# Hybrid attention and MLP on one core: double places for dequantized pieces, layer norm by turns with them, and zero products beside the first block's last maxima

## The chip, the cores and the metric

The kernel runs on one core of one Trainium2 chip. The metric is the device time of one execution in microseconds (us), the median of several. Before the change it is 1871.18 us (three runs, 1871.15 to 1873.65).

A core has five engines that run side by side, each with its own queue of instructions in a fixed order: PE (matrix products, with its weight loads PEld beside them), DVE (vectors), ACT (activations), POOL (vectors, and the issue of some DMAs) and SP (issue of DMAs). They wait for each other by semaphores. Products land in PSUM, from which DVE and ACT read.

## The reference

A layer stack on x of 2048 rows and 256 columns, in float32. The same packed MLP weights are used twice:

```python
x = x + attn_a(layernorm(x), Wq, bq, Wk, bk, Wv, bv, Wo, bo)   # rotary, 16 heads, 4 key heads, causal
x = x + ffn(layernorm(x), gate, up, down)
x = x + attn_b(layernorm(x), Wq, Wk, Wv, Wo)                   # 16 heads, causal
x = x + ffn(layernorm(x), gate, up, down)

def ffn(x, ...):                 # weights: 4-bit codes, two in an int32, times a scale per 32
    Wg, Wu, Wd = dequant_nvfp4(...)               # value = LUT[code] * scale
    gate, up = x @ Wg.T, x @ Wu.T                 # 2048 features
    gelu = tanh(0.79788 * (gate + 0.044715 * gate**3)) * gate * 0.5 + gate * 0.5
    return (gelu * up) @ Wd.T
```

Softmax is computed with the maximum of each row subtracted, so a row's maxima over all its keys must be known before its exponentials.

## The kernel before, in words

**Stages.** First attention, MLP, second attention, MLP. The 2048 rows are four blocks b of 512 rows. An attention goes through 16 units (b, g): block b of queries, group g of four heads, in the order (0,0), (0,1) ... (3,3). Unit n computes the values (exponentials and products with v) of its own queries, and beside them the row maxima of unit n+1.

**A unit's main steps** come from value_steps (L819): for each of 4(b+1) tiles of keys kt two pairs p. pair (L845) puts the scores of two heads into a ps_s buffer: two matmuls L853 that add the negative maxima mT, two matmuls L858 with the keys; on the diagonal a mask (L733), held back until the next step that settles it (settle, L738); then ACT's exp (L870). values (L824) multiplies the exponentials of the tile before with v (L838) into ps_av. There are three ps_s buffers, one ps_av and one ps_m.

**Its side steps** are woven between the main steps (weave, L43; blend, L61, merges two lists by their relative places). They are:
- the maxima of the next unit (max_steps, L747): for each step a pair of matmuls L758 into a ps_s buffer, and DVE's reduction L770; on the diagonal a mask held back in the same way. Then gather (L782 to L793, DVE) and at the unit's end turn: four matmuls L806 into ps_m, which ACT copies to mT (L812). For units up to (1,0) turn begins with four matmuls of zeros into ps_m that nobody reads (L802).
- the out projection of the block before (out_steps, L912) and the preparation of the block after (prep_steps, L438: layer norm, projections, rotary sums on POOL at L519, key loads issued by POOL at L705, query loads issued by SP at L719).
- in the first attention, `extra`: dequantizing, 72 steps, shared out over units 4 to 15 (none to those with g = 3 but the last). Units 4, 5 and 6 get 6, 5 and 5 steps, units 8 to 10 get 6, 5 and 5, units 12 to 14 get 6, 5 and 5, and the last unit, which has no maxima, gets 24.
- in the last unit, `beside`: 13 steps of layer norm for the first block of the MLP (Mlp.prep_steps, L1003): four of statistics (L295, L296 on DVE), one root (L300 on DVE, L302 on POOL), four norms (L310, DVE), four turns (two PE transposes L1016 into ps_m, an ACT copy L1017). They stand behind all of `extra`. The second attention has no `extra`, so there they stand alone.

**Dequantizing** is in 12 pieces (dequant_steps, L319): eight for gate and up, which go straight to wg and wu in SBUF, and four for down, which go to DRAM (wd_kept). A piece is six steps of unpack (L323):
1. load: SP loads the codes dq_q (L330), POOL issues eight loads of the scales dq_s (L339).
2. lowest: POOL copies the low bytes of dq_q to dq_b (L344).
3. and 4. move 0 and move 1: DVE takes dq_b apart (L355, L357 or L359, L361).
5. and 6. scaled 0 and scaled 1: DVE multiplies with dq_s (L370); for a down piece the last one also issues a store on SP (L399).

Every tile of the pool has one buffer. So the load of piece i waits on SP until lowest of piece i-1 has read dq_q, and on POOL until scaled 1 of piece i-1 has read dq_s.

**The MLP** begins with the matmuls L1040 on the turned layer norm xnT and the weights wg and wu. Its down weights wd are loaded from wd_kept (L1032) and used after the 16 feature steps of a block.

Of the kernel before, what the change touches and what calls it, by code (L numbers as in the profile page):

```python
# [9 lines left out]
F32 = mybir.dt.float32  # L10
# [4 lines left out]
I32 = mybir.dt.int32  # L15
# [6 lines left out]
P = 128  # L22
# [8 lines left out]
TB = 512  # L31
# [29 lines left out]
def blend(a, b):  # L61

    keyed = [((n + 0.5) / len(a), 0, n, f) for n, f in enumerate(a)]
    keyed += [((n + 0.5) / len(b), 1, n, f) for n, f in enumerate(b)]
    return [f for *_, f in sorted(keyed, key=lambda k: k[:3])]


def cut(steps, n):

    while 0 < n < len(steps) and getattr(steps[n - 1], "open", False):  # L70
        n += 1
    return steps[:n], steps[n:]
# [8 lines left out]
def tile_hybrid_layers(  # L81
# [25 lines left out]
    nc = tc.nc  # L107
# [20 lines left out]
    def ps_m():  # L128
        return psum.tile([P, 512], F32, tag="m", name="ps_m")
# [59 lines left out]
    nothing = const.tile([P, TB], BF16, tag="nothing", name="nothing")  # L189
    nc.vector.memset(nothing, 0.0)  # L190
    sel = const.tile([P, 2, P], BF16, tag="sel", name="sel")
# [127 lines left out]
    def dequant_steps(pool):  # L319

        def unpack(src, scale, results, done):  # L323
            held = {}
            n = TB // 4
            mag, sgn = 0x1C1C1C1C, 0x80808080

            def load():
                q = pool.tile([P, TB], I32, tag="dq_q", name="dq_q")
                nc.sync.dma_start(out=q, in_=src) if len(src.shape) == 2 else nc.sync.dma_start(  # L330
                    out=q.rearrange("p (c h) -> p c h", h=D), in_=src
                )
                s = pool.tile([P, TB], F32, tag="dq_s", name="dq_s")
                for r in range(8):
                    rows = s[16 * r : 16 * (r + 1), :]
                    row = scale(r)
                    if len(row.shape) == 3:
                        rows = rows.rearrange("p (c h) -> p c h", h=D)
                    nc.gpsimd.dma_start(out=rows, in_=row.broadcast_to(list(rows.shape)))  # L339
                held["q"], held["s"] = q, s  # L340

            def lowest():
                b8 = pool.tile([P, TB], U8, tag="dq_b", name="dq_b")
                nc.gpsimd.tensor_copy(  # L344
                    b8, held["q"].bitcast(U8).rearrange("p (n k) -> p n k", k=4)[:, :, 0]
                )
                held["w"] = b8.bitcast(U32)

            def move(k):

                w = held["w"]
                t = pool.tile([P, n], U32, tag=f"dq_t{k}", name="dq_t")
                v = pool.tile([P, n], U32, tag=f"dq_v{k}", name="dq_v")
                shift = (ALU.logical_shift_left, ALU.logical_shift_right)[k]
                nc.vector.tensor_scalar(t, w, 2, mag, shift, ALU.bitwise_and)  # L355
                if k == 0:
                    nc.vector.tensor_scalar(v, w, 4, sgn, shift, ALU.bitwise_and)  # L357
                else:
                    nc.vector.tensor_scalar(v, w, sgn, None, ALU.bitwise_and)  # L359
                e = pool.tile([P, n], U32, tag=f"dq_e{k}", name="dq_e")  # L360
                nc.vector.tensor_tensor(e, t, v, ALU.bitwise_or)  # L361
                held[k] = e

            def scaled(k):
                to = results()[k]
                code, sc = held[k].bitcast(FP8), held["s"]
                if len(to.shape) == 3:
                    code = code.rearrange("p (c h) -> p c h", h=D)
                    sc = sc.rearrange("p (c h) -> p c h", h=D)
                nc.vector.scalar_tensor_tensor(to, code, 64.0, sc, ALU.mult, ALU.mult)  # L370
                if k == 1 and done:
                    done()

            return [
                load, lowest, lambda: move(0), lambda: move(1), lambda: scaled(0), lambda: scaled(1)
            ]

        steps = []
        for k in range(MLP // TB):
            cols = slice(k * TB, (k + 1) * TB)  # L380
            for src, sc, w in ((gate_p, gate_s, wg), (up_p, up_s, wu)):
                steps += unpack(
                    src[:, cols], lambda r, sc=sc, cols=cols: sc[r : r + 1, cols],
                    lambda w=w, cols=cols: (w[:, 0, cols], w[:, 1, cols]), None,
                )
        d_p = down_p.rearrange("(c p) h -> p c h", p=P)
        d_s = down_s.rearrange("(c r) h -> r c h", r=8)
        for k in range(4):
            cc = slice(2 * k, 2 * k + 2)
            held = {}  # L390

            def results(held=held):
                if not held:
                    held["t"] = pool.tile([P, 4, D], F32, tag="dq_d", name="dq_d")
                w = held["t"].rearrange("p (c b) h -> p b c h", b=2)
                return w[:, 0], w[:, 1]

            def done(held=held, k=k):
                nc.sync.dma_start(out=wd_kept[:, 4 * k : 4 * k + 4, :], in_=held["t"])  # L399

            steps += unpack(
                d_p[:, cc, :], lambda r, cc=cc: d_s[r : r + 1, cc, :], results, done
            )
        return steps


    class Attention:
# [535 lines left out]
        def run(self, extra, beside):  # L943


            units = [(b, g) for b in range(NB) for g in range(NG)]


            room = [0 if n < NG else 9 if n + 1 == len(units) else 2 * (g < 3 or b + 1 == NB)
                    for n, (b, g) in enumerate(units)]  # L950
            shares = [-(-len(extra) * sum(room[: n + 1]) // sum(room)) for n in range(len(units))]
            given, ending, ahead = 0, [], []
            for n, (b, g) in enumerate(units):
                lead, more = [], []
                if g == 0 and b > 0:
                    more += self.out_steps(b - 1)
                if g == 0 and b + 1 < NB:
                    ahead = self.prep_steps(b + 1)

                    third = len(ahead) / 3  # L960
                    few = [round(third) - (1 if b else 2), round(third) + 1, len(ahead)]
                if g < 3 and b + 1 < NB:
                    part, ahead = cut(ahead, few[g])
                    if g == 2:

                        part[6:6] = [lambda b=b: self.load_q(b + 1, 0)]
                    more += part
                if shares[n] > given:
                    more = blend(more, extra[given : shares[n]])
                    given = shares[n]  # L970
                if n == 0 and self.after:
                    lead, more = self.after[:2], self.after[2:] + more
                elif n + 2 < len(units) and g != 2:
                    self.load_q(*units[n + 2])
                maxima, turn = [], None
                if n + 1 < len(units):
                    maxima, turn = self.max_steps(*units[n + 1])
                else:
                    more += beside
                steps, end, divide = self.value_steps(b, g)  # L980

                for at, step in zip((0, 2), ending):
                    scored, *summed = steps[at] if isinstance(steps[at], tuple) else (steps[at],)
                    steps[at] = (scored, step, *summed)
                if turn:
                    scored, summed = steps[-1]
                    steps[-1] = (turn, scored, summed)
                first = len(maxima) * 3 // len(steps)
                weave(steps[:3], lead + maxima[:first])
                weave(steps[3:], blend(maxima[first:], more) if maxima else more, rest=3)  # L990
                ending = [end, divide]
            end()
            return [divide] + self.out_steps(NB - 1)
# [93 lines left out]
    with tc.tile_pool(name="wk1", bufs=2) as wk, tc.tile_pool(name="kv1", bufs=1) as kv:  # L1087
        at.wk = at.qpool = wk
        with tc.tile_pool(name="init", bufs=1) as pool:
            zeros = pool.tile([P, TB], BF16, tag="zeros", name="zeros")  # L1090
# [13 lines left out]
            steps, turn = at.max_steps(0, 0)  # L1104
# [12 lines left out]
        with tc.tile_pool(name="dq", bufs=1, reuse_waits="tile") as pool:  # L1117
            left = at.run(dequant_steps(pool), mlps[0].prep_steps(0))
    first_w.close()
    at = Attention(False, wqkv_second)  # L1120
    with tc.tile_pool(name="kv20", bufs=1, reuse_waits="tile") as kv0, tc.tile_pool(
        name="wk2", bufs=2, reuse_waits="tile"
# [7 lines left out]
        steps, turn = at.max_steps(0, 0)  # L1130
# [60 lines left out]
```

## Time and profile before

| what | us |
|---|---|
| median of three runs | 1871.18 |
| the profiled execution: its own time | 1874.91 |
| the profiled execution: span from first to last instruction | 1873.1 |
| busy: PE / DVE / ACT / POOL | 1779.5 / 1124.8 / 806.5 / 240.3 |
| mean granted PE clock (1 is full) | 0.983 |
| DVE's reductions for the maxima, L770, 640 of them | 659.0 |
| exponentials, L870, 640 of them | 571.5 |
| first attention: unit (0,3) / last unit, from the L806 matmuls before it | from 107.40 / from 572.67 |
| second attention: unit (0,3) / last unit, from the L806 matmuls before it | from 1039.76 / from 1490.07 |

How to read it: a timeline row gives start, length, engine, line, operation, output and inputs with sizes, and how often; brackets give the engine's idle time just before and what ended it. A row of a stretch gives its length, then the busy time of PE, PEld, DVE, ACT and POOL with the number of instructions, then the granted PE clock, the share of DMA and GB/s. PE's matmuls overlap, so its busy time is an upper estimate. All times are us from the start of the span.

### The profile page before, as it was taken

What the parts mean: (1) busy time and instruction counts of PE and PEld (TensorE: products, weight loads), DVE (VectorE), ACT (ScalarE), POOL (GpSimd) and SP (SyncE); (2) the same over time, 40 slices, a digit from 0 to 9 for tenths busy, and PEclk for the clock granted to TensorE, in tenths of its full rate; (3) what the DMA queues carried; (4) which work ended last, traced back from release to release, by engine and by line L of the source; (5) the groups of instructions that cost most, each with busy time, mean ns of one, the idle gap of its engine ahead of it and who ended that gap; (6) DMA issues with size and microseconds to landing.
All of it is one profiled execution on the core that took longest, in us unless ns stands there. A gap on an engine that the chain in (4) does not pass through costs nothing. (4 is left out here: it accounts for less than half of the span.)

```text
span 1873.1 us, 31992 instructions
## 1 busy us (share of the span) xinstructions
PE 1779.5 (95%) x13534; PEld 929.9 (50%) x13534; DVE 1124.8 (60%) x1679; ACT 806.5 (43%) x1071; POOL 240.3 (13%) x444
## 2 busy tenths in 40 slices
PE   8889999999999899999998899999999999999999
PEld 4444444444443465747464444444444444756656
DVE  4567787788884444363545667766877716353442
ACT  2334556556667322132314355565566663131221
POOL 4121201200003111012101010010000001011110
PEclk9879999999999899999999899999999999999999
DMA  5131300200002100003104122022000010000000
GB/s 136 52 80 24 86 24 24 63 24 24 19 12 75 57 6 1 1 0 77 47 0 91 46 57 69 13 63 63 13 13 2 1 46 1 12 3 9 6 6 12
DMA packets 41887, 63.45 MB, mean 34 GB/s; under 512 B 13712, under 2 KB 20752, under 8 KB 41488
## 3 DMA queue, kind: packets, MB, share of 16 engines
q1 hardware_dynamic: 33104, 45.41, 7.9%
q0 software_dynamic: 7680, 15.48, 4.9%
q8 instruction: 106, 1.74, 0.4%
q10 hardware_dynamic: 960, 0.52, 0.1%
q14 instruction: 37, 0.30, 0.1%
HBM read 43.45 MB, written 17.83 MB: 33 GB/s over the span
## 5 line engine op out<-in xcount | busy, mean ns | idle before, releaser
L770 DVE TENSOR_REDUCE mx<-ps_s 128x2 f32<-128x1024 f32 (+3 forms) x640 | 659.0, 1061 | 224.0 <-PE ps_s L733 116.5
L870 ACT ACTIVATE e<-ps_s 128x1024 f32<-128x1024 f32 (+3 forms) x640 | 571.5, 897 | 412.9 <-PE ps_s L858 234.0
L838 PE MATMUL ps_av<-e,v 128*32 128x256 f32 (+1 forms) x4608 | 366.8, 387 | 0.4 <-ACT e L870 0.4
L858 PE MATMUL ps_s<-qT,kT 64*128 64x512 f32 (+3 forms) x1280 | 339.4, 523 | 0.0
L758 PE MATMUL ps_s<-kT,qT 64*128 64x512 f32 (+3 forms) x1280 | 269.0, 425 | 32.2 <-ACT e L870 14.3
L853 PE MATMUL ps_s<-mT,sel 64*128 64x512 bf16 (+3 forms) x1280 | 231.2, 355 | 27.5 <-ACT mT L812 11.0
L1040 PE MATMUL ps_s<-xnT,wg 128*128 128x512 f32 x512 | 240.9, 593 | 0.0
L1040 PE MATMUL ps_s<-xnT,wu 128*128 128x512 f32 x512 | 240.6, 592 | 0.0
L853 PEld LDWEIGHTS <-sel 64*128 64x128 bf16 x1280 | 74.9, 93 | 253.7 <-issue 243.3
L758 PEld LDWEIGHTS ps_s<-kT,qT 64*128 64x128 f32 x1280 | 129.4, 189 | 137.7 <-ACT e L870 67.6
L1046 ACT ACTIVATE t<-ps_s 128x512 f32<-128x512 f32 x128 | 76.3, 596 | 244.2 <-PE ps_s L1040 243.7
L1048 DVE TENSOR_TENSOR t<-ps_s,t 128x512 f32<-128x512 f32 x128 | 88.1, 688 | 141.2 <-POOL t L1047 139.2
L1049 ACT ACTIVATE t<-t 128x512 f32<-128x512 f32 x128 | 80.6, 629 | 198.9 <-DVE t L1048 198.9
L1040 PEld LDWEIGHTS ps_s<-xnT,wu 128*128 128x128 f32 x512 | 97.3, 190 | 122.5 <-issue 122.5
L1047 POOL TENSOR_SCALAR t<-t 128x512 f32<-128x512 f32 x128 | 79.1, 618 | 548.0 <-ACT t L1046 544.4
L1040 PEld LDWEIGHTS ps_s<-xnT,wg 128*128 128x128 f32 x512 | 95.1, 190 | 104.2 <-issue 102.5
L838 PEld LDWEIGHTS ps_av<-e,v 128*32 128x32 f32 x4608 | 94.9, 109 | 104.2 <-issue 87.9
L1050 DVE SCALAR_TENSOR_TENSOR t<-t,ps_s 128x512 f32<-128x512 f32 x128 | 88.0, 687 | 89.0 <-ACT t L1049 89.0
L858 PEld LDWEIGHTS ps_s<-qT,kT 64*128 64x128 f32 x1280 | 129.8, 198 | 0.0
L1065 PE MATMUL ps_m<-wd,inter 128*128 128x256 f32 x512 | 114.5, 380 | 0.0
L1065 PE MATMUL ps_av<-wd,inter 128*128 128x256 f32 x512 | 114.5, 380 | 0.0
L1065 PEld LDWEIGHTS ps_av<-wd,inter 128*128 128x128 f32 x512 | 96.7, 190 | 17.1 <-issue 4.5
(145 smaller groups left out, 1206.6 us busy)
## 6 DMA issues: line engine op xcount, KB each, us to landing
qT<-h SPq DMA_DIRECT2D x248, 64.0 KB, 2.2
kT<-h POOLq DMA_DIRECT2D x88, 128.0 KB, 5.0
h<-high SPq DMA_DIRECT2D x24, 256.0 KB, 2.1
h<-low SPq DMA_DIRECT2D x24, 256.0 KB, 2.4
wd<-wd_kept SPq DMA_DIRECT2D x2, 2048.0 KB, 8.2
wd_kept<-dq_d SPq DMA_DIRECT2D x4, 512.0 KB, 2.7
out<-x SPq DMA_DIRECT2D x16, 128.0 KB, 1.7
x<-x SPq DMA_DIRECT2D x3, 512.0 KB, 7.8
```

The source lines that it names most:

```text
L758: nc.tensor.matmul(pt[:, r, :w], lhsT=self.qT[b, g][64 * r : 64 * r + 64, p, i * P : (i + 1) * P], rhs=self.key_rows(c, g, p, r, slice(0, w)),
L770: nc.vector.tensor_reduce(held["mx"][:, i, 2 * p : 2 * p + 2, c], pt[:, :, :w], AX.X, ALU.max)
L838: nc.tensor.matmul(held["av"][32 * j : 32 * j + 32, own], lhsT=self.vv[kt // NT][:, kt % NT, h * VW : h * VW + 32], rhs=es_[j // 2][:, j % ...
L853: nc.tensor.matmul(pt[:, r, q0:], lhsT=sel[64 * r : 64 * r + 64, p, :], rhs=self.mT[b, g][64 * r : 64 * r + 64, q0:], start=True, stop=False,)
L858: nc.tensor.matmul(pt[:, r, q0:], lhsT=self.key_rows(kt // NT, g, p, r, keys), rhs=self.qT[b, g][64 * r : 64 * r + 64, p, q0:], start=Fals ...
L870: nc.scalar.activation(e[:, :, q0:], pt[:, :, q0:], AF.Exp, scale=QK_SCALE)
L1040: nc.tensor.matmul(pt[:, k, :], lhsT=w[:, c, fc * P : (fc + 1) * P], rhs=self.xnT[b][:, c, :], start=(c == 0), stop=(c == 1),)
L1047: nc.gpsimd.tensor_scalar(t, t, GELU_A, 1.0, ALU.mult, ALU.add)
L1048: nc.vector.tensor_tensor(t, gate, t, ALU.mult)
L1049: nc.scalar.activation(t, t, AF.Tanh, scale=GELU_C)
L1050: nc.vector.scalar_tensor_tensor(t, t, 1.0, gate, ALU.add, ALU.mult)
L1065: nc.tensor.matmul(po[:, :D], lhsT=inter[:, fc, i * P : (i + 1) * P], rhs=wd[:, fc, :], start=(fc == 0), stop=(fc == NFC - 1),)
```

## The change

Three edits, all in how side steps are made and ordered.

1. dq_q and dq_s get two buffers each (4 KB more per partition), and dequant_steps no longer strings the pieces one after another: the load of piece i+1 is put ahead of lowest of piece i. There are still 72 steps, shared out as before, so every step but the loads moves back by one place. Load of piece i+1 now waits for piece i-1 to be done with its buffer.
2. In the last unit of an attention, layer norm (`beside`) is merged with the dequantizing steps by blend, not appended. In the second attention there is nothing to merge with.
3. In unit (0,3) of both attentions, eight steps `zeros` are merged among the 16 maxima of unit (1,0): each takes ps_m and does two matmuls of 128 by 512 zeros in bfloat16, which nobody reads. The four at L802 stay.

```diff
@@ unpack, load
-                q = pool.tile([P, TB], I32, tag="dq_q", name="dq_q")
+                q = pool.tile([P, TB], I32, tag="dq_q", name="dq_q", bufs=2)
...
-                s = pool.tile([P, TB], F32, tag="dq_s", name="dq_s")
+                s = pool.tile([P, TB], F32, tag="dq_s", name="dq_s", bufs=2)
@@ dequant_steps
-        steps = []
+        pieces = []
...
-                steps += unpack(
+                pieces.append(unpack(
...
+        steps = pieces[0][:1]
+        for piece, then in zip(pieces, pieces[1:] + [[]]):
+            steps += then[:1] + piece[1:]
         return steps
@@ Attention.run
+            def zeros():
+                pt = ps_m()
+                for _ in range(2):
+                    nc.tensor.matmul(
+                        pt, lhsT=sel[:, 0, :], rhs=nothing, start=True, stop=True
+                    )
...
                 else:
-                    more += beside
+                    more = blend(more, beside)
...
+                if (b, g) == (0, 3):
+
+                    maxima = blend(maxima[:-1], [zeros] * 8) + maxima[-1:]
                 first = len(maxima) * 3 // len(steps)
                 weave(steps[:3], lead + maxima[:first])
                 weave(steps[3:], blend(maxima[first:], more) if maxima else more, rest=3)
```

In the last unit of the first attention the order of the side steps was load 8, lowest 8, move, move, scaled, scaled, load 9 and so on to scaled 1 of piece 11, then layer norm. It is now scaled 1 of piece 7, statistics 0, load 9, lowest 8, statistics 1, move 0 of 8, move 1 of 8, statistics 2, scaled 0 of 8, statistics 3, scaled 1 of 8, load 10, root, lowest 9, move 0 of 9, norm 0, move 1 of 9, scaled 0 of 9, norm 1, scaled 1 of 9, load 11, norm 2, lowest 10, move 0 of 10, norm 3, move 1 of 10, scaled 0 of 10, turn 0, scaled 1 of 10, turn 1, lowest 11, move 0 of 11, turn 2, move 1 of 11, scaled 0 of 11, turn 3, scaled 1 of 11.

More of the change, by code (lines that the diff above doesn't have):

```diff
@@ L381, in dequant_steps @@
             for src, sc, w in ((gate_p, gate_s, wg), (up_p, up_s, wu)):
-                steps += unpack(
+                pieces.append(unpack(
                     src[:, cols], lambda r, sc=sc, cols=cols: sc[r : r + 1, cols],
                     lambda w=w, cols=cols: (w[:, 0, cols], w[:, 1, cols]), None,
-                )
+                ))
         d_p = down_p.rearrange("(c p) h -> p c h", p=P)
@@ L399, in done @@
                 nc.sync.dma_start(out=wd_kept[:, 4 * k : 4 * k + 4, :], in_=held["t"])
-            steps += unpack(
+            pieces.append(unpack(
                 d_p[:, cc, :], lambda r, cc=cc: d_s[r : r + 1, cc, :], results, done
-            )
+            ))
+        steps = pieces[0][:1]
+        for piece, then in zip(pieces, pieces[1:] + [[]]):
+            steps += then[:1] + piece[1:]
         return steps
```

## The prediction

> **What bounds the kernel now.** I read the page first, then where engines wait in the stretches that the change touches, then the timelines of PE and DVE there, then both last units side by side, and last the granted clock window by window.
>
> ```profile
> PE 1779.5 (95%) x13534; PEld 929.9 (50%) x13534; DVE 1124.8 (60%) x1679; ACT 806.5 (43%) x1071; POOL 240.3 (13%) x444
> ```
>
> PE sets the end nearly everywhere, so an edit pays only where PE idles or runs at a low clock. There are two such places in reach of the change. The first is the end of the first attention's last unit, block 3, group 3 (PE, timeline):
>
> ```profile
> 604.93 0.47 PE L858 MATMUL ps_s<-qT,kT 64*128 64x384 f32 x2
> 611.93 0.70 PE L1016 MATMUL ps_m<-ident,xn 128*128 128x128 f32 x2 [6.53 <-DVE xn L310]
> ...
> 623.66 1.98 PE L1040 MATMUL ps_s<-xnT,wg 128*128 128x512 f32 x4
> ```
>
> PE idles 6.53 us for a layer-norm result of DVE. DVE's timeline says why it is late:
>
> ```profile
> 587.33 0.23 DVE L355 TENSOR_SCALAR dq_t<-dq_b 128x128 uint32<-128x128 uint32 x1 [7.33 <-POOL dq_b L344]
> 596.10 0.23 DVE L355 TENSOR_SCALAR dq_t<-dq_b 128x128 uint32<-128x128 uint32 x1 [6.08 <-POOL dq_b L344]
> 605.28 0.23 DVE L355 TENSOR_SCALAR dq_t<-dq_b 128x128 uint32<-128x128 uint32 x1 [6.14 <-POOL dq_b L344]
> 607.89 0.42 DVE L295 BATCH_NORM_STATS2 stats<-x 128x6 f32<-128x256 f32 x1
> ...
> 611.47 1.38 DVE L310 TENSOR_SCALAR xn<-x,mv,rstd 128x256 f32<-128x256 f32 x4 [1.16 <-POOL rstd L302]
> ```
>
> Three pieces of dequantizing each hold DVE for 6 to 7 us, and all of layer norm stands behind the last. The second attention's last unit does the same PE work with layer norm alone beside it. It is the twin to measure by. Both stretches run from the first L806 matmul (the turned maxima) to the first L1040 matmul; after the span come PE busy, PEld, DVE, ACT and POOL, then the clock:
>
> ```profile
> 572.67:623.66 50.99, 43.19 (x433) 16.92 (x433) 14.20 (x47) 32.48 (x39) 14.80 (x28) 0.87 0.22 74
> 1490.07:1530.22 40.15, 39.35 (x436) 16.11 (x433) 4.23 (x15) 32.42 (x39) 1.03 (x1) 1.00 0.15 54
> ```
>
> 10.84 us of difference: the idle time, and the half clock that follows it. The second place is unit (0,3), in both attentions (the same columns):
>
> ```profile
> 109.68:113.09 3.41, 1.93 (x25) 1.05 (x24) 3.41 (x4) 2.08 (x3) 0.00 (x0) 1.00 0.42 112
> 113.09:116.50 3.41, 3.41 (x20) 1.70 (x22) 3.03 (x3) 0.68 (x2) 0.00 (x0) 0.50 0.06 16
> 116.50:119.92 3.42, 1.99 (x26) 1.02 (x18) 3.12 (x5) 0.87 (x2) 0.00 (x0) 1.00 0.00 0
> 119.92:130.15 10.23, 10.05 (x99) 5.28 (x100) 7.29 (x14) 2.08 (x4) 0.00 (x0) 0.50 0.01 2
> 1041.51:1044.92 3.41, 2.33 (x28) 1.21 (x26) 3.14 (x3) 1.56 (x3) 0.00 (x0) 1.00 0.49 144
> 1044.92:1048.33 3.41, 2.89 (x28) 1.39 (x27) 3.32 (x4) 1.21 (x2) 0.00 (x0) 1.00 0.01 4
> 1048.33:1051.75 3.42, 1.75 (x18) 0.89 (x16) 3.36 (x5) 0.87 (x2) 0.00 (x0) 1.00 0.01 2
> 1051.75:1061.99 10.24, 10.06 (x99) 5.29 (x100) 7.29 (x14) 2.08 (x4) 0.00 (x0) 0.50 0.01 2
> 27.76:31.17 3.41, 2.63 (x28) 1.48 (x28) 2.54 (x5) 0.29 (x1) 3.41 (x11) 1.00 1.10 214
> ```
>
> The clock changes only at steps of 3.41 us counted from 31.17. Cut on that grid, from 27 us on and up to the last 6 us, every window at full clock with PE busy 60% or less is followed by one at half (57%, 58% and 51% above), and none from 65% up is, but one (77%, the last row). In unit (0,3) DVE is the full engine, with reductions of 1.17 us; PE waits for it, the clock falls, and then for 10.2 us PE at half clock is the bound.
>
> **Layer norm by turns with dequantizing: -10.84 us.** I wrote out the new order of the unit by the rules of blend and weave, and timed DVE and POOL from rows. DVE is free at 577.34. It now starts with the last scaling of piece 7 (half of a 1.30 row: 577.99). POOL's eight loads of scales for piece 9 wait for that, as loads wait today (579.99 to 580.29: 0.30), and take 3.97: 582.27. The copy of the low bytes of piece 8 follows (0.61: 582.88). DVE then runs the two moves of piece 8 (587.33 to 588.73: 1.40), two scalings (1.30) and the two layer-norm statistics in between (0.53 each), to 586.7; the other two statistics ran before, under the loads. Loads for piece 10 end at 590.95, and behind them on POOL come rstd (1.04) and the copy for piece 9: 592.6. The first norm (0.35) is done at 593.6, the second at 595.4, the third at 596.4. Loads for piece 11, the copy for piece 10 and one move bring the fourth to 601.9. PE wants them later: in the twin its four turns stand 26.60, 29.28, 32.03 and 34.93 us after the start, and here each is one pair (1.2) earlier in the order: 598.1, 600.8, 603.5 and 606.4. So the least slack is 4.5 us, no turn waits, and the unit takes the twin's 40.15.
>
> One thing does not go: the chain scaling, loads, copy, move still stands, since the load of piece i+1 waits for the scaling of piece i-1 and the copy of piece i is issued behind it on POOL. The second place removes only the wait for codes (POOL waited 4.8 us for them in three steps). DVE still waits some 4 us per piece; layer norm merely no longer stands behind all of it. What is late next is the last scaling (606.8) and its store on SP; the load of wd (623.81 today) follows the end of the unit, and its first use is the whole first feature loop later, so it costs nothing.
>
> **Loads a piece sooner in units 4 to 14: 0 us.** DVE waited for a copy three times in all, each in the last unit, so there is no stall to win earlier. POOL issues the same 96 loads and SP the same 12, earlier by one piece. Two pieces stand on POOL at 103.12 where one stood; POOL was then idle until 138.43, so 3.9 us more fit. Where rotary sums stand on POOL (L519; ACT's cast waits for them) the new loads come behind the sum that is due, not ahead of it, in units 6 and 9; in unit 5 they are ahead of one, at about 170 where it was due at 185.8. On SP the loads stand behind query loads that wait for a buffer (27.05 us at 108.10), as now, with a piece in hand. DVE work shifts by one step: unit 4 loses 0.68, unit 10 gains 0.65, unit 14 loses 0.68 and the last unit takes it under the loads. PE sets those units, so I take 0; were DVE the bound, -1.4 to +0.7.
>
> **Zero products in unit (0,3): -2.9 us.** Eight pairs, one to every two maxima. At full clock four such matmuls took 0.87 (81.17 to 82.04), so a pair is 0.43. A window holds 2.9 reductions, so 1.45 pairs: +0.63 us or 18 points. 57, 58 and 51% become 75, 76 and 70%, over the 65% from which the clock stayed. I take it that it stays, and followed the second attention's unit with full-clock steps (pair 0.45, maximum 0.10 to 0.35, mask 0.16, values 0.57, reductions as they are). The price of the pairs shows on DVE: the mask of the pair ahead, and so its exp and the buffer that it frees, comes 0.43 later (DVE idles 0.2 and 0.15); the fourth zero pair waits until the division has read ps_m (0.4 on PE; behind it stands the next maximum, which DVE, still at the one before, does not yet want); and on the diagonal a maximum's mask is issued behind the zero pair that follows it, so DVE, now with short reductions, idles 0.7, 0.65 and 0.25. The gather ends at 1061.3, the L806 matmuls start at 1061.5 instead of 1062.72: -1.2. The first attention took 23.48 for what took 22.96 here (107.40 to 130.88, 1039.76 to 1062.72); at the same new length it gains 0.5 more: -1.7. Bounds: with no idle DVE time from 1041.78 the rows add to 17.57 and the gather ends at 1059.35, which gives -3.2 and -3.7, -6.9 together. Above, if the clock falls as now, the last four pairs of each pass stand on the bound at half clock, 0.97 each (31.20 to 32.17): +3.9 a pass, +7.8 together.
>
> [...]
>
> **Sum.** -10.84 - 2.9 + 0 = -13.7 us on the profiled execution (1874.91, span 1873.1): 1861.2. The three timed runs' median, 1871.18, lies 3.7 below that execution; I subtract the same from it: **1857.5 us**.
>
> **Rivals.** (1) The forecast: 55%. (2) The clock falls all the same. For it: the 77% window, which held zero products too and fell. In one pass: -10.84 - 1.5 + 3.9, **1862.7**, 17%. In both: -10.84 + 7.8, **1868.1**, within 0.2%: 10%. (3) The idle moves with the turns: if dequantizing runs 6 us later than I timed, the fourth norm is 1.5 late and a thin window halves the clock for 3.4 us, some 3.5 lost: **1861**, 6%. Against it: 4.5 us of slack. (4) PE stays ahead and DVE never idles: **1853.4**, 7%. (5) Slower: unit (0,3) sits at half clock from its first maxima in both passes, so that all 16 pairs at 0.97 are PE's bound: +15.5 - 10.84, **1875.9**, 5%. It decides from the point where windows such as 1041.51 and 1044.92 (68 and 85% busy before zeros are added) fall too, which speaks against it.
>
> 0.2% is 3.7 us, about what a measurement tells from no change. Faster by more: 85%; within: 10%; slower: 5%. Range: 1853.4 less 1.4 to 1868.1 plus 0.7, **1852.0 to 1868.8**.
>
> **What would show it.** Right: no wait of PE on L310 in the last unit, about 40.2 us from L806 to L1040, DVE still waiting some 4 us on the copy; clock 1.00 through both units (0,3), and L806 21.7 us after the one before. Wrong: a turn that waits for a norm, or a 0.50 window among the zero products.

## The result, and the profile after

The changed kernel takes **1860.07 us** (median of six runs, 1858.8 to 1861.01) where the kernel before, in six runs beside it, takes 1870.57 (1866.93 to 1873.65). The ratio is 0.9943 (95% interval 0.9929 to 0.9956), so it is 10.5 us faster. The profiled execution took 1859.89, its span is 1857.8, and its mean granted clock is 0.994 (before: 1873.1 and 0.983).

First the page's busy times of the changed kernel. Its lines behind the dequantizing have moved: before's L733, L758, L770, L806 and L858 are now L737, L762, L774, L810 and L862, L1016 is L1031, and L1040 is L1055.

```profile
PE 1774.0 (95%) x13566; PEld 925.0 (50%) x13566; DVE 1125.1 (61%) x1679; ACT 806.8 (43%) x1071; POOL 241.1 (13%) x444
```

PE has 32 matmuls more and is busy 5.5 us less, because fewer of them run at half clock: by the mean clocks of 0.994 and 0.983, some 22 us of the span now and some 64 before. DVE, ACT and POOL do what they did. The next rows are stretches of the changed kernel (columns as in the prediction): the last unit of the first attention, from the turned maxima (L810) to the first matmul of the MLP (L1055), and unit (0,3) of the first and the second attention, from its turned maxima to the next unit's.

```profile
570.32:610.46 40.14, 39.34 (x436) 16.10 (x432) 14.86 (x48) 32.45 (x39) 15.56 (x29) 1.00 0.26 87
106.59:128.93 22.34, 20.07 (x206) 9.18 (x204) 17.31 (x23) 6.60 (x10) 3.47 (x8) 1.00 0.20 39
1025.22:1047.82 22.60, 20.10 (x205) 9.19 (x204) 17.30 (x23) 6.60 (x10) 0.00 (x0) 1.00 0.08 25
```

The last unit takes 40.14 where it took 50.99, and 40.14 is also what the second attention's last unit takes. The two units (0,3) run at full clock, and take 22.34 and 22.60 where they took 23.48 and 22.96.

PE's timeline of the last unit in the changed kernel shows the four turns of layer norm and the first matmul of the MLP. No row has an idle time behind it in brackets:

```profile
596.91 0.51 PE L1031 MATMUL ps_m<-ident,xn 128*128 128x128 f32 x2
...
599.60 0.50 PE L1031 MATMUL ps_m<-ident,xn 128*128 128x128 f32 x2
...
602.35 0.50 PE L1031 MATMUL ps_m<-ident,xn 128*128 128x128 f32 x2
...
605.24 0.50 PE L1031 MATMUL ps_m<-ident,xn 128*128 128x128 f32 x2
...
610.46 1.98 PE L1055 MATMUL ps_s<-xnT,wg 128*128 128x512 f32 x4
```

DVE's timeline of the same stretch shows why. The norms (L310) now stand among the pieces of dequantizing:

```profile
580.61 0.23 DVE L355 TENSOR_SCALAR dq_t<-dq_b 128x128 uint32<-128x128 uint32 x1 [3.85 <-POOL dq_b L344]
...
590.40 0.23 DVE L355 TENSOR_SCALAR dq_t<-dq_b 128x128 uint32<-128x128 uint32 x1 [5.86 <-POOL dq_b L344]
...
591.01 0.41 DVE L310 TENSOR_SCALAR xn<-x,mv,rstd 128x256 f32<-128x256 f32 x1
...
594.01 0.41 DVE L310 TENSOR_SCALAR xn<-x,mv,rstd 128x256 f32<-128x256 f32 x1
...
599.09 0.23 DVE L355 TENSOR_SCALAR dq_t<-dq_b 128x128 uint32<-128x128 uint32 x1 [4.67 <-POOL dq_b L344]
599.70 0.41 DVE L310 TENSOR_SCALAR xn<-x,mv,rstd 128x256 f32<-128x256 f32 x1
...
605.12 1.29 DVE L370 SCALAR_TENSOR_TENSOR dq_d<-dq_e,dq_s 128x512 f32<-128x512 fp8e4 x2 [1.61 <-DMA wd_kept<-dq_d]
```

DVE still waits 3.85, 5.86 and 4.67 us for POOL's copy. These waits no longer hold a norm that PE wants: the first norm starts at 591.01 and its turn at 596.91, the fourth at 599.70 and 605.24. The last row is a new wait, of DVE for the store out of dq_d, which has one place. PE waits for none of it.

DVE's maxima of unit (0,3) in the second attention of the changed kernel show what the zero products cost:

```profile
1027.24 2.36 DVE L774 TENSOR_REDUCE mx<-ps_s 128x2 f32<-128x1024 f32 x2 [5.09 <-PE ps_s L762]
...
1029.96 2.36 DVE L774 TENSOR_REDUCE mx<-ps_s 128x2 f32<-128x1024 f32 x2 [0.37 <-PE ps_s L762]
1032.69 2.36 DVE L774 TENSOR_REDUCE mx<-ps_s 128x2 f32<-128x1024 f32 x2 [0.37 <-PE ps_s L762]
...
1036.14 2.36 DVE L774 TENSOR_REDUCE mx<-ps_s 128x2 f32<-128x1024 f32 x2 [0.47 <-PE ps_s L762]
1038.73 0.76 DVE L774 TENSOR_REDUCE mx<-ps_s 128x2 f32<-128x256 f32 x2 [0.23 <-PE ps_s L737]
...
1040.34 0.69 DVE L774 TENSOR_REDUCE mx<-ps_s 128x2 f32<-128x512 f32 x1 [0.85 <-PE ps_s L737]
...
1041.49 0.69 DVE L774 TENSOR_REDUCE mx<-ps_s 128x2 f32<-128x512 f32 x1 [0.46 <-PE ps_s L737]
1042.45 4.09 DVE L774 TENSOR_REDUCE mx<-ps_s 128x2 f32<-128x768 f32 x4 [0.26 <-PE ps_s L737]
```

DVE, the full engine of this unit, waits for PE before nearly every second maximum. After the first row (the start of the unit) the waits add to 0.37 + 0.37 + 0.47 + 0.23 + 0.85 + 0.46 + 0.26 = 3.01 us. PE's timeline has the pair that stands ahead of one of them; it starts at 1027.13, and the next matmul 0.54 later:

```profile
1027.13 0.61 PE L961 MATMUL ps_m<-nothing,sel 128*128 128x512 bf16 x2
1027.67 0.50 PE L762 MATMUL ps_s<-kT,qT 64*128 64x512 f32 x2
```

**Where the 15.3 us between the two profiled spans are.** Cut from turned maxima to turned maxima: 10.85 in the last unit; 1.14 and 0.36 in the two units (0,3); 1.29 in the second attention's unit (0,2) (24.65 to 23.36), 0.30 before the first turned maxima and 0.52 in the first unit, none of which the change touches; the remaining 0.8 in steps of at most 0.6 either way. The untouched stretches move by as much between two executions of one and the same kernel: in three profiles of before, the second attention's unit (0,2) takes 23.39 to 24.74, the first turned maxima come at 37.99 to 39.38, and the first unit takes 19.03 to 19.68.

### The profile page after: what moved, and what is told of

Same layout as the page of the kernel before. It is cut to its first block, busy times and chain, and to the rows that moved or that the text cites. A ratio compares the mean times of both kernels' runs of the same rounds, so it can differ in the third digit from the quotient of the medians.

```text
span 1857.8 us, 32028 instructions
## 1 busy us (share of the span) xinstructions
PE 1774.0 (95%) x13566; PEld 925.0 (50%) x13566; DVE 1125.1 (61%) x1679; ACT 806.8 (43%) x1071; POOL 241.1 (13%) x444
## 5 line engine op out<-in xcount | busy, mean ns | idle before, releaser
L774 DVE TENSOR_REDUCE mx<-ps_s 128x2 f32<-128x1024 f32 (+3 forms) x640 | 659.5, 1061 | 220.2 <-PE ps_s L737 114.8
L842 PE MATMUL ps_av<-e,v 128*32 128x256 f32 (+1 forms) x4608 | 361.5, 382 | 0.4 <-ACT e L874 0.4
L862 PE MATMUL ps_s<-qT,kT 64*128 64x512 f32 (+3 forms) x1280 | 336.8, 519 | 0.0
L762 PE MATMUL ps_s<-kT,qT 64*128 64x512 f32 (+3 forms) x1280 | 266.4, 419 | 30.8 <-ACT e L874 15.3
L1055 PE MATMUL ps_s<-xnT,wg 128*128 128x512 f32 x512 | 240.9, 593 | 0.0
L1055 PE MATMUL ps_s<-xnT,wu 128*128 128x512 f32 x512 | 240.6, 592 | 0.0
L762 PEld LDWEIGHTS ps_s<-kT,qT 64*128 64x128 f32 x1280 | 127.4, 185 | 138.7 <-ACT e L874 67.0
L1055 PEld LDWEIGHTS ps_s<-xnT,wu 128*128 128x128 f32 x512 | 97.3, 190 | 122.5 <-issue 122.5
L1055 PEld LDWEIGHTS ps_s<-xnT,wg 128*128 128x128 f32 x512 | 95.1, 190 | 104.2 <-issue 102.5
L862 PEld LDWEIGHTS ps_s<-qT,kT 64*128 64x128 f32 x1280 | 128.6, 196 | 0.0
```

The source lines that it names most:

```text
L762: nc.tensor.matmul(pt[:, r, :w], lhsT=self.qT[b, g][64 * r : 64 * r + 64, p, i * P : (i + 1) * P], rhs=self.key_rows(c, g, p, r, slice(0, w)),
L774: nc.vector.tensor_reduce(held["mx"][:, i, 2 * p : 2 * p + 2, c], pt[:, :, :w], AX.X, ALU.max)
L842: nc.tensor.matmul(held["av"][32 * j : 32 * j + 32, own], lhsT=self.vv[kt // NT][:, kt % NT, h * VW : h * VW + 32], rhs=es_[j // 2][:, j % ...
L862: nc.tensor.matmul(pt[:, r, q0:], lhsT=self.key_rows(kt // NT, g, p, r, keys), rhs=self.qT[b, g][64 * r : 64 * r + 64, p, q0:], start=Fals ...
L1055: nc.tensor.matmul(pt[:, k, :], lhsT=w[:, c, fc * P : (fc + 1) * P], rhs=self.xnT[b][:, c, :], start=(c == 0), stop=(c == 1),)
```

## The experiments

The first theory was the prediction's: the order in the last unit gives nearly all, the places give nothing, and the zero products hold the clock and give a little. Its rivals were that the places already end the stall (a quicker chain of pieces), and that the zero products are worth nothing or more than forecast. Later, when one profile's clock had turned out to differ from the next, a second question came up: how much of each stretch is the kernel, and how much the place where the clock's windows fall. Kernels of one group shared a chip and the runs of the kernel before (medians 1871.09, 1869.53 and 1871.51 us in the three groups, 17 to 23 runs each, 1863.61 to 1875.99 over all). Ratios are to these runs, with 95% intervals; they are estimated from all of them and need not be the quotient of the medians. "Unit (0,3)" is given as first / second attention.

**No zero products: edits 1 and 2.**

```diff
-                if (b, g) == (0, 3):
-                    maxima = blend(maxima[:-1], [zeros] * 8) + maxima[-1:]
```

> The change without the zero products. Theory (the order of layer norm is the whole gain): the last unit of the first attention takes 40.1 us from the turned maxima to the first MLP matmul, as in the changed kernel, and the time is 10.9 us below the kernel before, within 1 us of the changed kernel; unit (0,3) shows half clock again and 22.5 to 23.5 us. Rival (the zero products carry a part): about 3 us slower than the changed kernel, 8 us below before.

Measured: 1861.93 us (1859.5 to 1866.74), ratio 0.9955 [0.9939, 0.9972]. Last unit 40.17; unit (0,3) 23.49 / 21.88. The median is 9.2 us below the kernel before, between the 10.9 of the theory and the 8 of the rival, so it does not decide between them; the last unit is as short as the theory wanted. The stretches of unit (0,3) in this kernel:

```profile
105.92:129.41 23.49, 19.80 (x189) 10.88 (x189) 17.12 (x23) 6.59 (x10) 3.45 (x8) 0.71 0.15 39
1025.83:1047.71 21.88, 17.91 (x189) 9.76 (x188) 17.11 (x23) 6.60 (x10) 0.00 (x0) 0.84 0.10 26
```

The clock falls in both, but in the second for some 7 us only, and that unit is then quicker at 0.84 than the changed kernel's is at 1.00 (22.60). The clock alone does not decide.

**The zero products alone: edit 3.**

```diff
+                if (b, g) == (0, 3):
+                    maxima = blend(maxima[:-1], [zeros] * 8) + maxima[-1:]
```

> The kernel before with the zero products alone. Theory: clock 1.00 through both units (0,3), 22.3 to 22.6 us each as in the changed kernel, so 1.5 us less at most against a profile with half clock there; the median moves by 0 to -1.5 us. Rival as predicted blind: -2.9 us. Second rival (zero products cost more PE time than the clock gives): +1 to +4 us.

Measured: 1870.43 us (1866.21 to 1872.1), ratio 0.9998 [0.9987, 1.0008]: nothing. The clock holds in both units, as it should, with 22.44 / 22.62; the stall in the last unit is there, but smaller than in the profile before (columns as above):

```profile
108.38:130.82 22.44, 19.70 (x202) 9.31 (x204) 17.31 (x23) 6.60 (x10) 0.00 (x0) 0.99 0.09 24
1035.76:1058.38 22.62, 19.64 (x203) 9.20 (x204) 17.30 (x23) 6.60 (x10) 0.00 (x0) 1.00 0.09 24
572.37:621.11 48.74, 41.89 (x432) 16.47 (x433) 14.19 (x47) 32.45 (x39) 14.81 (x28) 0.89 0.23 78
```

**The order alone: edit 2, with the kernel before's single places and loads.**

```diff
-                    more += beside
+                    more = blend(more, beside)
```

> The kernel before with layer norm by turns alone: one place for codes and scales, loads where they were. Theory: by the same chain the fourth norm is ready near 601 and its turn wants it near 606, so the last unit takes 40.1 us all the same: -10.9 us. Rival (the second place is what frees DVE): DVE's waits of 6 to 7 us per piece reach the turns, PE idles, the unit takes 45 us or more: -6 us or less.

Measured: 1864.35 us (1862.6 to 1865.14), ratio 0.9963 [0.995, 0.9977]. The last unit takes 40.15, as the theory wanted, but the median fell by 6.7 us and not by 10.9. The last unit as a stretch:

```profile
572.23:612.38 40.15, 39.35 (x433) 16.12 (x433) 14.12 (x47) 32.43 (x39) 14.87 (x28) 1.00 0.29 94
```

DVE's timeline of the last unit in this kernel:

```profile
587.57 0.23 DVE L355 TENSOR_SCALAR dq_t<-dq_b 128x128 uint32<-128x128 uint32 x1 [5.67 <-POOL dq_b L344]
...
595.65 0.23 DVE L355 TENSOR_SCALAR dq_t<-dq_b 128x128 uint32<-128x128 uint32 x1 [4.33 <-POOL dq_b L344]
...
605.44 0.23 DVE L355 TENSOR_SCALAR dq_t<-dq_b 128x128 uint32<-128x128 uint32 x1 [6.31 <-POOL dq_b L344]
```

DVE still waits 16.3 us for the copies in these three rows, where it was 19.6 before, and the unit is as fast as the changed kernel's. So the waits as such were not the cost; that layer norm stood behind them was. The profiled span, 1862.5, is 8.3 to 10.6 us below the three of the kernel before (1873.1, 1870.8 and 1872.4), which agrees with a last unit 10 us shorter. It is 4.8 above that of edits 1 and 2 (1857.7). Of this, 4.5 lie in stretches that neither edit touches and that vary in the kernel before as well: the start, both units (0,3), and units (0,0) and (0,2) of the second attention.

**The places alone: edit 1, with layer norm behind the dequantizing as before.**

```diff
-                    more = blend(more, beside)
+                    more += beside
```

(and no zero products)

> The kernel before with two places and loads a piece sooner alone; layer norm stays behind all pieces. Theory: a piece takes 7.6 us instead of 9.1 on DVE, the last scaling ends near 603.5 instead of 608, the first turn is 4.5 us earlier; PE still idles some 2 us and the clock still falls: -4 to -5 us. Rival (places change nothing, since POOL's loads still wait for the scaling): 0. Second rival (with the second place the stall goes altogether): -10.9.

Measured: 1869.61 us (1865.49 to 1880.24), ratio 0.9997 [0.9981, 1.0012]; last unit 49.58. DVE's timeline of the last unit in this kernel:

```profile
580.94 0.23 DVE L355 TENSOR_SCALAR dq_t<-dq_b 128x128 uint32<-128x128 uint32 x1 [4.92 <-POOL dq_b L344]
...
588.52 0.23 DVE L355 TENSOR_SCALAR dq_t<-dq_b 128x128 uint32<-128x128 uint32 x1 [4.92 <-POOL dq_b L344]
...
596.13 0.23 DVE L355 TENSOR_SCALAR dq_t<-dq_b 128x128 uint32<-128x128 uint32 x1 [4.92 <-POOL dq_b L344]
...
603.05 1.29 DVE L370 SCALAR_TENSOR_TENSOR dq_d<-dq_e,dq_s 128x512 f32<-128x512 fp8e4 x2 [2.23 <-DMA wd_kept<-dq_d]
```

The places do what they should: a piece now takes 7.6 us (580.94 to 588.52 to 596.13) where it took 8.8 to 9.2. But the unit starts with one scaling more, and the pieces, now quicker than the store, meet a new wait for the one place of dq_d (2.23). PE's row of the first turn in this kernel still has a stall:

```profile
608.31 0.70 PE L1021 MATMUL ps_m<-ident,xn 128*128 128x128 f32 x2 [4.90 <-DVE xn L310]
```

The forecast of 4 to 5 us was wrong. Some 2 us of idle time were expected here; it is 4.90, since this turn comes 37.6 us into the unit where it came 39.3 before, 1.6 earlier and not 4.5. With the half clock behind it (608.4 to 618.6) the unit is 1.4 us shorter than in the profile of before, and within what that unit shows from run to run. The rival that places suffice falls, too; the one that they change nothing in the time is not refuted.

**The change again, and without zero products again,** on another chip, since the two stood close.

> The changed kernel once more, to stand beside the next three on one chip. Units (0,3) at 22.3 and 22.6 us, no half clock in them, last unit 40.1 us; 9.5 to 11 us below the kernel before.

> The change without the zero products, beside the change on one chip. Theory (the zero products buy steadiness, not time: 22.3 and 22.6 us always, against 21.7 to 23.5 by the phase of the clock windows): the median within 1.5 us of the change, with a wider spread of the runs. Rival (they are worth what was predicted): the change faster by 2.9 us.

Measured: the change 1860.84 us (1860.6 to 1863.59), ratio 0.9970 [0.9958, 0.9982], unit (0,3) 22.48 / 22.72. The units came as expected, but the gain did not: 9.5 to 11 us were expected, and it is 8.7 between the medians and 5.6 by the ratio. The kernel without zero products took 1861.55 (1858.71 to 1863.12), 0.9967 [0.9955, 0.9980], unit (0,3) 21.79 / 22.80. The two can't be told apart. The second kernel also shows that the share of a window does not settle what the clock does. Rows of single clock windows (3.41 us, cut on this execution's own steps); of each two neighbours the first is the window, the second what followed:

```profile
93.56:96.97 3.41, 1.78 (x6) 0.47 (x4) 1.89 (x3) 0.62 (x1) 0.83 (x1) 1.00 1.05 125
96.97:100.39 3.42, 3.04 (x38) 2.50 (x38) 2.22 (x5) 1.12 (x2) 2.95 (x4) 1.00 0.56 167
114.04:117.45 3.41, 2.54 (x42) 1.76 (x42) 3.20 (x6) 0.81 (x1) 0.00 (x0) 1.00 0.00 0
117.45:120.86 3.41, 3.38 (x40) 1.83 (x36) 2.96 (x4) 0.60 (x1) 0.00 (x0) 0.50 0.02 5
```

A window with PE busy 52% (1.78 of 3.41) is followed by full clock, one with 74% (2.54 of 3.41) by half.

**Four zero pairs, each behind the step's maxima and masks,** where no mask waits for them.

```diff
-                    maxima = blend(maxima[:-1], [zeros] * 8) + maxima[-1:]
+                    for at in range(4):
+                        had = steps[at] if isinstance(steps[at], tuple) else (steps[at],)
+                        steps[at] = (*had, lambda: (self.settle(), zeros()))
```

> The change with four pairs of zero products, not eight, each at the end of one of the first four main steps of unit (0,3), behind the held-back masks, and none among the maxima on the diagonal. Theory (the price of the zero products is that they stand ahead of masks): the gaps of DVE before every second reduction (0.36) and on the diagonal (0.85, 0.46, 0.26) go, the clock stays at 1.00, and each unit takes 21.7 to 21.9 us: 1 us less than the change. Rival (the gaps come from PE's work as such): 22.3 and 22.6 as in the change. Second rival (four pairs do not hold the clock): half clock in at least one of the two units.

Measured: 1864.91 us (1862.08 to 1867.2), ratio 0.9978 [0.9966, 0.9990]; unit (0,3) 23.51 / 23.82, clock 0.92 and 0.86. DVE's maxima in the first attention of this kernel come first, then PE's row of the third zero pair:

```profile
111.10 7.06 DVE L774 TENSOR_REDUCE mx<-ps_s 128x2 f32<-128x1024 f32 x6 [5.19 <-PE ps_s L762]
...
120.16 2.69 DVE L774 TENSOR_REDUCE mx<-ps_s 128x2 f32<-128x1024 f32 x3 [1.38 <-PE ps_s L762]
```

PE's row:

```profile
118.84 0.60 PE L961 MATMUL ps_m<-nothing,sel 128*128 128x512 bf16 x2 [1.24 <-DVE att L904]
```

DVE's first six maxima run without a gap, with one pair to every two maxima as in the change, so the gaps of the change do come from pairs that stand ahead of masks. But the third pair now stands right behind the division, waits 1.24 us for its ps_m, and holds the next maximum (1.38). And four pairs do not hold the clock: it is at half from 123.0 to 126.4 in the first attention, and from 1041.2 to 1048.0 in the second.

**Eight zero steps of four matmuls, not two.**

```diff
-                for _ in range(2):
+                for _ in range(4):
```

> The change with four matmuls of zeros in each of the eight steps, not two. Theory (a pair costs its 0.54 us on PE wherever PE's next work is wanted by DVE): 16 matmuls more a pass, eight times 0.54 us; each unit (0,3) takes 25 to 26 us, the kernel 5 to 8 us more than the change. Rival (zero products lie beside DVE): 22.3 to 23 us, no change.

Measured: 1866.83 us (1860.98 to 1868.77), ratio 0.9984 [0.9973, 0.9995]; unit (0,3) 24.93 / 24.76, which is 2.5 and 2.0 more than in the change beside it. Two DVE rows of the first attention:

```profile
113.78 1.23 DVE L774 TENSOR_REDUCE mx<-ps_s 128x2 f32<-128x1024 f32 x1 [0.53 <-PE ps_s L762]
...
125.39 0.69 DVE L774 TENSOR_REDUCE mx<-ps_s 128x2 f32<-128x512 f32 x1 [1.29 <-PE ps_s L737]
```

What was 0.37 is 0.53, what was 0.85 is 1.29: the zero products sit on the path, at some 0.3 us (2.5 / 8) for each added pair, of the 0.54 that it takes. The units account for 4.5 of the 6.0 us by which this kernel's median stands over the change's.

**Four pairs, among the first eight maxima only.**

```diff
-                    maxima = blend(maxima[:-1], [zeros] * 8) + maxima[-1:]
+                    maxima = blend(maxima[:8], [zeros] * 4) + maxima[8:]
```

> The change with four pairs of zero products, among the first eight maxima of unit (1,0) only, none on the diagonal. Theory (on the diagonal a pair stands ahead of a mask that DVE waits for, and PE is busy enough there without it): DVE's gaps of 0.85 and 0.46 go, the clock stays, units of 21.6 to 22.1 us, 1 us less than the change. Rival (the windows on the diagonal need the pairs): half clock there in one or both units, 22.5 to 23.5 us, no better than the change.

Measured: 1863.91 us (1860.07 to 1868.62), ratio 0.9962 [0.9946, 0.9977]; unit (0,3) 22.40 / 23.94. Windows of the second attention in this kernel:

```profile
1043.12:1046.53 3.41, 2.35 (x44) 1.67 (x44) 2.52 (x5) 0.90 (x2) 0.00 (x0) 1.00 0.02 5
1046.53:1049.94 3.41, 3.00 (x34) 1.77 (x34) 3.19 (x5) 0.51 (x1) 0.00 (x0) 0.50 0.00 0
```

The window on the diagonal, without its pairs, is busy 69% and the clock falls after it. In the first attention it held (22.40), so four early pairs held the clock in one pass of two.

**Eight zero steps of one matmul.**

```diff
-                for _ in range(2):
+                for _ in range(1):
```

> The change with one matmul of zeros in each of the eight steps, not two. Theory (a pair costs DVE its gaps, the clock is kept by PE's busy share of a 3.41 us window, over some 61 to 65%): gaps before the reductions shrink to some 0.1, units of 21.8 to 22.1 us where the clock stays; the thinnest window (51% before) comes to some 60% and may fall in one of the two units, which then takes 22.5 to 23 us. Rival: the clock stays in both and the kernel is 1 us under the change.

Measured: **1859.65 us** (1857.59 to 1862.77), ratio 0.9941 [0.9922, 0.9961]; span of its profile 1855.8. Its stretches of unit (0,3):

```profile
106.80:128.08 21.28, 18.54 (x195) 9.62 (x196) 17.38 (x23) 6.69 (x10) 2.30 (x5) 0.98 0.14 37
1024.37:1045.82 21.45, 18.21 (x194) 9.24 (x196) 17.39 (x23) 6.60 (x10) 0.00 (x0) 1.00 0.10 26
```

And DVE's maxima in the first attention of this kernel:

```profile
109.07 2.36 DVE L774 TENSOR_REDUCE mx<-ps_s 128x2 f32<-128x1024 f32 x2 [5.21 <-PE ps_s L762]
111.58 4.86 DVE L774 TENSOR_REDUCE mx<-ps_s 128x2 f32<-128x1024 f32 x4 [0.16 <-PE ps_s L762]
...
120.81 0.69 DVE L774 TENSOR_REDUCE mx<-ps_s 128x2 f32<-128x512 f32 x1 [0.49 <-PE ps_s L737]
```

The unit itself is at full clock (the 0.98 of the first row is the end of an earlier fall). DVE's gaps behind the first row add to 1.11 us, where they are 2.73 in this unit of the change, and the units are 1.06 and 1.15 us shorter than in the change. They are the shortest pair of any profile here, and shorter than the 21.8 to 22.1 that were expected. The thinnest window, for which some 60% was expected, is busy 73%:

```profile
111.25:114.66 3.41, 2.50 (x17) 1.09 (x16) 3.11 (x4) 1.24 (x2) 0.00 (x0) 1.00 0.27 78
```

Over the whole kernel it is ahead of the change by 0.4 to 1.2 us of median, which these runs do not separate. That one matmul is enough rests on this one profile.

**The kernel before, profiled twice more.** Nothing is edited.

> The kernel before, one more profile. Theory (the clock's windows run free, so what the stall in the last unit costs depends on where the window edge falls): last unit between 48.7 and 51.0 us, units (0,3) between 21.7 and 23.5, and a time between 1863 and 1875. Rival (the profile that the forecast used is typical): 50.99, 23.48 and 22.96 again.

> The same once more, for another window edge: last unit between 48.7 and 51.0 us by the theory, 50.99 by the rival.

Measured: 1872.58 and 1874.2 us in the profiled executions. The last unit in the first of them, as a stretch:

```profile
570.31:620.44 50.13, 43.82 (x433) 17.11 (x433) 14.19 (x47) 32.47 (x39) 14.79 (x28) 0.86 0.23 75
```

The other:

```profile
571.62:622.28 50.66, 43.52 (x432) 16.97 (x433) 14.20 (x47) 32.49 (x39) 14.82 (x28) 0.87 0.23 74
```

PE's idle time ahead of the first norm was 5.05 and 5.87 us, where the profile of before had 6.53. The table collects the stretches that differ, in us:

| | last unit, first attention | unit (0,3), first / second | unit (0,2), first / second |
|---|---|---|---|
| before, shown above | 50.99 | 23.48 / 22.96 | 25.36 / 24.65 |
| before, a second time | 50.13 | 21.78 / 22.96 | 26.82 / 24.74 |
| before, a third time | 50.66 | 21.78 / 22.73 | 26.78 / 23.39 |
| zero products alone | 48.74 | 22.44 / 22.62 | 26.83 / 23.36 |
| places alone | 49.58 | 22.09 / 21.71 | 25.33 / 23.36 |
| order alone | 40.15 | 23.45 / 23.01 | 25.35 / 24.65 |
| no zero products, twice | 40.17, 40.13 | 23.49 / 21.88, 21.79 / 22.80 | 25.30 / 23.39, 22.57 / 24.89 |
| the change, twice | 40.14, 40.15 | 22.34 / 22.60, 22.48 / 22.72 | 25.36 / 23.36, 25.31 / 23.38 |
| one zero matmul a step | 40.16 | 21.28 / 21.45 | 26.46 / 23.37 |

The two units of the first attention have to be read together. The 21.78 of two profiles of before is no gain: unit (0,2) is longer there, and both units add to 48.84, 48.60 and 48.56 in the three.

## Why the prediction was right

**Layer norm by turns (-10.84): the mechanism holds, the size is that of one execution.** With the order alone the last unit takes 40.15, and with the change 40.14 and 40.15; no turn waits. My timing of DVE and POOL was close: counted from the start of the unit, I had the norms done at 20.9, 22.7, 23.7 and 29.2 us, and they are done at about 21, 23, 24 and 30. The turns came at 26.6, 29.3, 32.0 and 34.9, the twin's own places and not one pair sooner, so the least slack is some 5 us rather than 4.5. That DVE would go on waiting is right too, for 4.8 us a piece in the mean and not some 4 (3.85, 5.86, 4.67). What was mis-sized is the start of the subtraction. The unit with before's order and places took 50.99, 50.13, 50.66 and 48.74 in four profiles, 50.13 in the mean, so the edit is worth about 10.0 us of a typical execution; I had priced it by the costliest of the four. Edit 2 alone (6.7 us of median, 0.9963) falls short of that. In the one profile of it the difference lies in stretches that the edit does not touch; why all its six runs (1862.6 to 1865.14) should be so is not shown.

**A load a piece sooner (0): right.** Units 4 to 14 together take 441.4 us with the places (the change, and without zero products) and 441.8, 441.5 and 441.4 without them (the three profiles of before). Single units shift by up to 0.6 us and give it back. Alone, the places give 0.9997 [0.9981, 1.0012]. I named the chain of scaling, loads, copy and move as what remains; I did not name the store. dq_d has one place, and DVE waits for it 1.61 us in the change and 2.23 with the places alone. The last scaling ends 36.1 us into the unit and not, as I had it, 34.1, at no cost to PE.

**Zero products (-2.9): the step that was mis-sized; -1.5 between the two profiles, and about nothing on average.** That the clock holds is right in every profile with eight steps. The 75, 76 and 70% that I worked out came to 80 to 100% in the first profile of the change, and to no less than 76% in the second. Two terms failed. The first is the price on DVE: a pair takes 0.54 of PE, not 0.43, and DVE's gaps add to 3.01 us where I listed 0.2, 0.15, 0.7, 0.65 and 0.25, 1.95 together. The unit so takes 22.60, not 21.7. The second is the other side of the subtraction: without zero products the unit took 23.48, 23.49, 23.45, 22.09, 21.79, 21.78 and 21.78 in the first attention, 22.55 in the mean, and 22.96, 21.88, 23.01, 21.71, 22.80, 22.96 and 22.73 in the second, 22.58. With them it took 22.42 and 22.65 in the mean of three profiles. That is 0.1 us in all. With unit (0,2) of the first attention added, which varies from 22.57 to 26.83 us though no edit touches it, the means of the same profiles are 47.9 without and 48.3 with them, again no gain. Both agree with the 0.9998 of the zero products alone. What they buy is a steady unit (0,3): 22.3 to 22.7 every time.

**The rule of 65%: a tendency only.** On the one trace I had, from 27 us on, windows up to 60% were always followed by half clock, and from 65% up all but one by full. On other executions a window of 52% was not, and windows of 69 and 74% were (rows above). Which window falls where differs from execution to execution: the steps of the clock lie on a grid of 3.41 us in each trace, but at 3.37, 1.52, 2.91 and 1.40 us from the start of the span in the change, the two later profiles of before, and the second one without zero products. Nor did it take a long idle stretch for the clock to fall: no idle stretch of PE in the units (0,3) was over 1.3 us, and the clock fell in all fourteen without zero products and in three of the four with four pairs. That eight zero steps hold it (1.00 in both units of the change) speaks against my second rival.

**The subtraction from the median.** I took the same 13.7 from the median as from the profiled execution, which lay 3.7 above it. The profiles differ by 15.0 (1874.91 to 1859.89), the medians by 10.5, and about 10.0 + 0.1 is what the unit means of the table give. So the profile of before was a costly execution, and part of what I took from it was not in the median: 13.7 less 10.1 is 3.6, more than the 2.6 us between 1857.5 and 1860.07. Repeated on another chip the change gave 0.9970 [0.9958, 0.9982], an interval that does not meet the first one (0.9929 to 0.9956). By these ratios the gain is 5.6 and 10.7 us, so its size is known to some 5 us only. That it is a gain, and that it comes from layer norm, does not hang on this; the forecast of the direction rested on that one term.

**The rivals.** The clock held in both passes, so the first two fell. Layer norm was not late, so the third fell; that the measured 1860.07 lies nearer to its 1861 than to 1857.5 is chance. PE did not stay ahead: DVE idles 3 us, so the fourth fell, and even one matmul a step leaves 21.28, where this rival wanted 19.8 (23.48 - 3.7). The slower case needed windows such as 1041.51 and 1044.92 to fall with zeros in them; none did.

**What stays open.** What beyond the share of a window decides on the clock; why the two measurements of the change differ by more than their intervals; how much one matmul a step gains over two in the whole kernel; and why the three profiled executions of before (1874.91, 1872.58 and 1874.2) all lie above its medians, while those of the change (1859.89 and 1860.6) do not.

## What to carry to other kernels

Where an engine waits several times in a row, look first at what stands in order behind the waits: with work of another kind put between them, the waits can stay nearly as long as they are, and cost nothing (with the order alone DVE waits 16.3 us in three rows, in a unit of 40.15). A stall that also lowers the clock had no fixed price here (48.74 to 50.99 us for the unit that holds it, at a mean clock of 0.86 to 0.89, in four profiles): take it from several executions of the same kernel, as the mean of a stretch, before you subtract it. Zero products that held the clock were work on the path of DVE, which waited for PE (0.54 us of PE a pair, 3.01 us of gaps on DVE), and with two matmuls a step they gained nothing (0.9998 alone); if you use them, use the fewest that hold it (here eight times one matmul, in one profile), along the whole thin stretch (four pairs among the first eight maxima let the clock fall in one pass of two), and not right behind an instruction that still reads their buffer (a pair that stood so waited 1.24 us).

## What was not expected of the hardware

- **One kernel's time varies with the clock that it is granted.** 23 runs of the kernel before on one chip went from 1863.61 us, at a mean granted clock of 0.992, to 1875.13, at 0.982 (0.6%). Between its three profiles only a few stretches differ: the start and unit (0,0), units (0,2) and (0,3), the last unit, and the start of the second attention. Every other unit agrees within 0.2 us. That the phase of the clock's windows makes the difference fits these profiles, whose steps lie at different places, but no run sets it. The changed kernel, with the stall and the thin units gone, went from 1858.8 to 1861.01 and from 1860.6 to 1863.59.
- **A higher mean clock is not a shorter unit.** In the second attention, unit (0,3) took 21.88 us at 0.84 without zero products, 22.60 at 1.00 with them.
- **The stall itself varies, too.** PE's idle time ahead of the same norm was 6.53, 5.05 and 5.87 us in three executions of one kernel, all for DVE's norm, whose time hangs on POOL's loads and copies (DVE waited 7.33, 6.08 and 6.14 us for the copies in the first of the three).
